# New announced durations for the list scheduler of the attention stage

## The chip, the cores and the metric

The kernel runs on one core of a Trainium2 chip, in one launch. The metric is the time on the device in microseconds (us). Lower is better. A core has a matrix engine (TensorE, PE in the profile), three engines for elementwise work (VectorE or DVE, ScalarE or ACT, GpSimd or POOL) and SyncE (SP), whose queue issues most of the transfers. Each engine works through its own queue of instructions in order, and they wait for each other by semaphores.

## The reference, cut to what matters

The input is x (16 batches of 1024 nodes with 128 features) and a 0/1 adjacency per batch. Four layers follow each other, each with a layer norm and a ReLU before it and a sum with x after it. Layer 0 thins out the adjacency row by row and applies three graph convolutions with batch norms. The other three are what the stage of this change computes:

```python
# layer 1: attention, 4 heads of 32; edges enter as log(adjacency)
scores = einsum('chqd,chkd->chqk', q, k) * SCALE + log(max(adj, EPS))
x = x + softmax(scores) @ v, projected by Wo
# layer 2: graph attention (GAT)
e = leaky_relu(s_i[i] + s_j[j]); e = where(adj > 1e-8, e, -1e9)
x = x + einsum('bijh,bihd->bjhd', softmax(e, axis=i), Wh)
# layer 3: graph convolution (GCN)
x = d^-1/2 (adj + I) d^-1/2 @ h @ W.T + b + x
```

## The kernel before, in words

A first stage thins out the adjacency, a second computes the convolutions of layer 0, and the last, `attentions_plain`, does layers 1 to 3. A slow path behind a test at the end is built into the program as well, and the test decides at run time that it is not entered.

`attentions_plain` is written as seven Python generators, each of which goes through the 16 batches:

- `matrices` loads the adjacency (tile a, from HBM by SP), turns it into fp8 (tile A, L1318 on ACT), checks on DVE that it holds 0 and 1 only (L1322) and on PE and ACT that it is symmetric (L1329 to L1335).
- `before` adds up the end of layer 0 from spilled rows (tiles h_a and hT_a, L1365 on PE, L1369 on DVE), normalizes (`normal`), transposes (`transposed`, L1291 on PE), and makes q, k (L1383) and v (`natural_times`, L1303).
- `attend` copies 16 times the adjacency into the score banks (tile t, four PSUM banks, one buffer; L1416 on ACT), multiplies the heads' keys and queries onto it (L1421 on PE) and takes the exponential in two halves (L1429 on ACT). This is done 16 times a batch.
- `values` multiplies the exponentials by v and by ones (L1452 on PE), 16 steps a batch; after each 8 it takes the reciprocal (L1458) and scales (oT, L1460, DVE). Then comes the output projection (L1303) and the sum with x (L1462).
- `positive` makes for each of the four heads a mask of the pairs with a positive score: the destination scores go out to HBM and come back spread over all partitions (tile dst), and DVE compares, 8 instructions a head (tile pm, L1503).
- `gat` normalizes, transposes, multiplies by W2 (L1523), makes the exponentials of the scores, splits the values into three bf16 parts (tiles vals and parts; POOL L1543, ACT L1549 and L1553, DVE L1551 and L1555), sums over A (L1563, 8 steps) and over the masks (L1578, 16 steps), with a DVE reduction after each (L1566, L1581), and combines the two (L1589 to L1598).
- `gcn` normalizes, splits into parts (L1615 to L1621), multiplies by A (L1632) and the identity (L1636), copies (aggT, L1639), projects (L1303) and stores the result.

Nobody writes the order of this work by hand. Before a step, a generator yields the engine, an announced duration, the planned time from which the step may start, and a change in the number of held PSUM banks of the pool "sum" (two banks). `in_order` keeps a planned free time for each engine and always takes the step with the smallest planned start, then those not on PE, then the generator with the least planned PE work done in relation to its share. The chosen generator is resumed and emits the instructions of its step. So the instructions of each queue, transfers included, stand in the order in which the planner took the steps. The core of it:

```python
engine, took, needs, _ = j["next"]
start = max([free[engine], needs] + [min(pools[pool]) for pool, change in tiles(j) if change > 0])
key = (start, engine == "PE", j["did"] / j["per"] + j["lag"])
...
end = free[engine] = start + took
...
j["next"] = j["job"].send(end + HOP)
```

HOP is 0.25. Nothing of the planned times is left in the program: no instruction waits for a clock. Two more things bind the order: `before` and `matrices` begin a batch only when `gcn` has finished the batch four earlier and `values` the one two earlier, and most tiles of `gat`, `gcn` and `before` have one buffer.

Of the kernel before, what the change touches and what calls it, by code (L numbers as in the profile page):

```python
# [1213 lines left out]
def attentions_plain(tc, x, spill, final, ready_weights, adj, deg, trouble, eye, out, scores, bound, reach):  # L1214
    nc = tc.nc
    with ExitStack() as ctx:
# [68 lines left out]
        def transposed(src, t, out):  # L1285

            for hf in range(2):
                e = yield "PE", 0.7, t, 1
                ps = bank()
                for c in range(4):  # L1290
                    nc.tensor.transpose(ps[:, c * P:(c + 1) * P], src[:, 4 * hf + c, :], ident)  # L1291
                e = yield "ACT", 0.6, e, -1
                nc.scalar.copy(out[:, hf * HN:(hf + 1) * HN], ps)
            return e

        def natural_times(xT, t, w, eng, finish):

            for hf in range(2):
                e = yield "PE", 1.05, t, 1
                ps = bank()  # L1300
                for c in range(4):
                    k = 4 * hf + c
                    nc.tensor.matmul(ps[:, c * P:(c + 1) * P], xT[:, k * P:(k + 1) * P], w, start=True, stop=True)  # L1303
                e = yield eng, 0.7, e, -1
                finish(slice(4 * hf, 4 * hf + 4), blocked(ps))
            return e

        def matrices():

            for b in range(B):  # L1310
                while done["gcn"] < b - 3 or done["attend"] < b - 1:
                    yield
                m = adp.tile([P, NB, N], F8, name="A")
                for i in range(NB):
                    t = yield "ACT", 1.3, 0.0, 0
                    a = lp.tile([P, N], F32, name="a")
                    nc.sync.dma_start(a, adj[b, i * P:(i + 1) * P, :])
                    nc.scalar.activation(m[:, i, :], a, AF.Relu, accum_out=deg[:, b, i:i + 1], saturate=False)  # L1318
                    yield "DVE", 1.4, 0.0, 0
                    junk = lp.tile([P, N], F8, name="junk", bufs=1)  # L1320

                    nc.vector.scalar_tensor_tensor(junk, a, 0.0, a, op0=ALU.is_gt, op1=ALU.not_equal,  # L1322
                                                   accum_out=trouble[:, b, i, 0:1], saturate=False)
                    for hf in range(2):
                        w = min(HN, (i - 4 * hf) * P)
                        if w > 0:
                            e = yield "PE", 0.1 + w / 1024, t, 1
                            ps = bank()
                            nc.tensor.matmul(ps[:, :w], ident16, m[:, i, hf * HN:hf * HN + w], start=True, stop=False)  # L1329
                            for j in range(w // P):  # L1330
                                nc.tensor.matmul(ps[:, j * P:(j + 1) * P], m[:, 4 * hf + j, i * P:(i + 1) * P], minus16,
                                                 start=False, stop=j == w // P - 1)
                            yield "ACT", 0.8, e, -1
                            junk = lp.tile([P, HN], BF16, name="junk2", bufs=1)
                            nc.scalar.activation(junk[:, :w], ps[:, :w], AF.Abs, accum_out=trouble[:, b, i, 1 + hf:2 + hf])  # L1335

                t = yield "DVE", 0.2, 0.0, 0
                nc.vector.tensor_scalar(dinv[:, b], deg[:, b], 1.0, None, op0=ALU.add)
                yield "POOL", 1.7, t, 0
                nc.gpsimd.tensor_tensor(dinv[:, b], dinv[:, b], minus_half, op=ALU.pow)  # L1340
                A[b] = m

        def before():

            for b in range(B):
# [6 lines left out]
                for hf in range(2):  # L1352
                    cols = slice(hf * HN, (hf + 1) * HN)
                    two = w1.tile([P, 2, HN], F32, name="h_a")
                    for l in range(2):
                        nc.sync.dma_start(two[:, l], spill[l, b][:, cols])
                    rows = [two[:, 0], two[:, 1], last[:, cols]]
                    for half in range(2):
                        e = yield "PE", 2.2, 0.0, 1 - half
                        if half == 0:  # L1360
                            ps = bank()
                            nc.tensor.matmul(ps, ones16, final[3][:, None, :].to_broadcast([3, 4, D]), start=True, stop=False)
                        for c in range(2 * half, 2 * half + 2):
                            for l in range(3):
                                nc.tensor.matmul(ps[:, c * P:(c + 1) * P], rows[l][:, c * P:(c + 1) * P], final[l],  # L1365
                                                 start=False, stop=c == 3 and l == 2)
                    t = yield "DVE", 0.7, e, -1
                    part = xt[:, 4 * hf:4 * hf + 4, :]
                    nc.vector.tensor_tensor(part, part, blocked(ps), op=ALU.add)  # L1369
                h = w1.tile([P, NB, D], F32, name="h_a")  # L1370
                t = yield from normal(xt, t, h)
                hT = w1.tile([P, N], F32, name="hT_a")
                t = yield from transposed(h, t, hT)
# [4 lines left out]
                for out_, w, bias, scale in ((qT, wq, bqc, qscale), (kT, wk_, bkc, 1.0)):  # L1378
                    for hf in range(2):
                        cols = slice(hf * HN, (hf + 1) * HN)  # L1380
                        e = yield "PE", 0.95, t, 1
                        ps = bank()
                        nc.tensor.matmul(ps, w, hT[:, cols], start=True, stop=True)  # L1383
                        e = yield "ACT", 0.7, e, -1
# [12 lines left out]
        def attend():  # L1397

            last = 0.0


            s = pss.tile([P, H, HN], F32, name="t")
            for hd in range(H):
                for c in range(4):
                    nc.tensor.matmul(s[:, hd, c * P:(c + 1) * P], ident16, ident16, start=c == 0, stop=c == 3)
            n = 0
            for b in range(B):
                while b not in ready or b not in A:
                    yield
                t, xt, qT, kT, va = ready[b]  # L1410
                for hf in range(2):
                    cols = slice(hf * HN, (hf + 1) * HN)
                    for k in range(NB):
                        e = yield "ACT", 1.9, last, 0

                        nc.scalar.activation(s, A[b][:, k, None, cols].to_broadcast([P, H, HN]), AF.Copy, scale=16.0)  # L1416
                        e = yield "PE", 1.1, max(e, t), 0

                        for hd in range(H):
                            r = slice(hd * HD, (hd + 1) * HD)  # L1420
                            nc.tensor.matmul(s[:, hd], kT[r, k * P:(k + 1) * P], qT[r, cols], start=False, stop=True,  # L1421
                                             skip_group_check=True)
                        while n > 1 and n - 2 not in taken:
                            yield
                        es = ep.tile([P, H, HN], F32, name="e")
                        e = max(e, taken.get(n - 2, 0.0))
                        for hd in range(0, H, 2):
                            e = yield "ACT", 1.07, e, 0
                            nc.scalar.activation(es[:, hd:hd + 2], s[:, hd:hd + 2], AF.Exp, scale=SIGMA)  # L1429
                        exps[n] = es, e  # L1430
                        last = e
                        n += 1

        def values():

            free, n = 0.0, 0
            for b in range(B):
                oT = w1.tile([P, N], F32, name="oT")
                for hf in range(2):
                    cols = slice(hf * HN, (hf + 1) * HN)  # L1440
                    for k in range(NB):
                        while n not in exps:
                            yield
                        es, e = exps[n]
                        e = yield "PE", 1.95, max(e, free), 0
                        if k == 0:
                            acc, den = [bank(psa, "acc") for _ in range(2)]
                        va = ready[b][4]
# [58 lines left out]
        def gat():  # L1507
            for b in range(B):
# [42 lines left out]
                nc.vector.tensor_tensor(v, v, parts[:, :, 0], op=ALU.subtract)  # L1551
                e = yield "ACT", 2.0, e, 0
                nc.scalar.copy(parts[:, :, 1], v)  # L1553
                t = yield "DVE", 2.4, e, 0
                nc.vector.tensor_tensor(parts[:, :, 2], v, parts[:, :, 1], op=ALU.subtract)  # L1555
                parts4 = parts.rearrange("p (c h) s w -> p c h s w", h=H)

# [11 lines left out]
                for hd in range(H):  # L1569
# [1 line left out]
                        yield  # L1571
                    pm, t = shared[b, hd]
                    for j in range(0, NB, 2):
                        e = yield "PE", 1.45, t, 1
                        ps = bank()
                        for jj in range(2):
                            for i in range(NB):
# [7 lines left out]
                shape = [P, NB, H, W]  # L1585
                t = yield "POOL", 3.1, e, 0
                nc.gpsimd.tensor_tensor(up, up, ex[:, 0, :, H:, None].to_broadcast(shape), op=ALU.mult)
                yield "DVE", 2.6, e, 0
                nc.vector.tensor_tensor(tot, tot, low, op=ALU.subtract)  # L1589
                nc.vector.tensor_tensor(tot, tot, ex[:, 1, :, H:, None].to_broadcast(shape), op=ALU.mult)  # L1590
                t = yield "DVE", 4.1, t, 0
# [10 lines left out]
        def gcn():  # L1602
            for b in range(B):
# [20 lines left out]
                for hf in range(2):  # L1624
                    cols = slice(hf * HN, (hf + 1) * HN)
                    for m in range(NB):
                        if m % 2 == 0:
                            e = yield "PE", 1.35, t, 0 if m else 1
                            if m == 0:
                                ps = bank()  # L1630
                        for k in range(3):
                            nc.tensor.matmul(ps, parts[:, k, m, :], A[b][:, m, cols], start=m == 0 and k == 0, stop=False)  # L1632
                    e = yield "PE", 0.8, t, 0
                    for m in range(4):
                        for k in range(3):
                            nc.tensor.matmul(ps[:, m * P:(m + 1) * P], parts[:, k, 4 * hf + m, :], ident16,  # L1636
# [191 lines left out]
```

## Time and profile before

| | us |
|---|---|
| median of 3 runs | 3990.11 |
| lowest, highest | 3984.71, 3998.74 |
| the profiled execution | 3983.57 |
| its span, first to last instruction | 3981.8 |

The mean granted clock of TensorE was 0.932 of full speed. On the page, PE is the matrix engine's multiplications and PEld its loads of the stationary operand, which overlap them. L with a number is a line of the kernel. In the timeline and the groups of instructions, `out<-in` gives the tiles by name, then the shapes, and x the number of instructions; brackets hold the idle time before and what ended it. In the list of waits the waiting engine, line and tile stand left of the arrow, and what it waited for stands right of it; the numbers are the total, the number of times and the longest. A table by stretches gives for each stretch the busy time of every engine, with the number of instructions in brackets, then the granted clock, the busy share of the transfer engines and GB/s.

### The profile page before, as it was taken

To read this page: it belongs to the slowest core of one execution; us is meant where nothing else is said; L and a number is where in the kernel's file an instruction comes from. 1 tells how busy PE (TensorE), PEld (TensorE's weight loads), DVE (VectorE), ACT (ScalarE), POOL (GpSimd) and SP (SyncE) were. 2 spreads that over 40 slices of the span, in tenths; PEclk is the share of its full clock that TensorE was granted. 3 is DMA by queue.
4 is the path that set the end of the run, shared out by engine and by line. 5 is a ranking of instruction groups with operands and counts; after the bars stand their busy time and mean duration, and the time that the engine had idled before them with its cause. 6 is when DMAs were issued, how large, how long until landed. Compare 5 with 4: busy or idle time off the path is not lost.

```text
span 3981.8 us, 65726 instructions
## 1 busy us (share of the span) xinstructions
PE 3429.2 (86%) x26692; PEld 1966.6 (49%) x26692; DVE 2528.4 (63%) x4782; ACT 2398.6 (60%) x3961; POOL 790.9 (20%) x680
## 2 busy tenths in 40 slices
PE   4888887899999986789899898998989899889775
PEld 2556565445555565335554544544444454454333
DVE  4988784553344444247775777677687686777656
ACT  3778764453333345776677676767757767776540
POOL 6545421210010011102121111111111101210110
PEclk9989986999999997999999998998999989999887
DMA  9632223443333314211221122122122112111000
GB/s 107 41 21 16 12 79 122 160 170 122 127 128 129 129 61 141 79 59 49 65 86 59 49 75 76 37 75 79 41 67 81 48 50 85 56 58 49 27 17 17
DMA packets 182499, 293.20 MB, mean 74 GB/s; under 512 B 77468, under 2 KB 124456, under 8 KB 173992
## 3 DMA queue, kind: packets, MB, share of 16 engines
q1 hardware_dynamic: 91944, 221.69, 17.1%
q0 software_dynamic: 79728, 24.66, 7.6%
q10 hardware_dynamic: 10512, 42.54, 2.7%
q8 instruction: 211, 3.46, 0.4%
q14 instruction: 104, 0.85, 0.1%
HBM read 287.98 MB, written 51.19 MB: 85 GB/s over the span
## 4 chain that ended last, share of the span: by engine, by line
PE 60%; DVE 20%; ACT 8%; DMA 5%; issue 3%; POOL 3%; ACTq 0%; SPq 0%; POOLq 0%; DVEq 0%
PE g L1040 12%; PE acc L1452 10%; PE sum L1578 9%; PE t L1421 5%; PE sum L1632 4%; PE sum L1563 4%; DVE pm L1503 3%; DMA rows<-in_adj_dram 2%; DVE rows L882 2%; PE sum L1365 2%; PE o L1089 2%; DVE r L835 2%; PE o L1090 2%; ACT e L1429 1%; PE sum L1383 1%
## 5 line engine op out<-in xcount | busy, mean ns | idle before, releaser
L1429 ACT ACTIVATE e<-t 128x1024 f32<-128x1024 f32 x512 | 507.9, 1022 | 485.8 <-PE t L1421 467.9
L1503 DVE SCALAR_TENSOR_TENSOR pm<-dst,minus,A 128x1024 fp8e4<-128x1024 f32 x512 | 675.5, 1348 | 8.4 <-DMA dst<-scores 8.3
L1040 PE MATMUL g<-C,parts 128*128 128x512 fp8e4 x2304 | 523.9, 382 | 15.9 <-DVE aggT L1042 10.0
L1416 ACT ACTIVATE t<-A 128x2048 f32<-128x2048 fp8e4 x256 | 482.0, 1883 | 3.9 <-ACT dst L1483 0.3
L1578 PEld LDWEIGHTS <-pm 128*128 128x128 fp8e4 x4096 | 346.6, 98 | 187.0 <-issue 165.0
L1578 PE MATMUL sum<-parts,pm 128*128 128x198 bf16 x4096 | 399.7, 251 | 26.1 <-DVE pm L1503 16.4
L1452 PE MATMUL acc<-e,va 128*32 128x512 f32 x2048 | 331.6, 620 | 41.1 <-ACT e L1429 38.2
L1040 PEld LDWEIGHTS <-parts 128*128 128x128 bf16 x2304 | 224.0, 99 | 264.1 <-issue 9.6
L1421 PE MATMUL t<-qT,kT 32*128 32x512 f32 x2048 | 303.5, 663 | 30.6 <-ACT t L1416 30.3
L1452 PE MATMUL acc<-e,ones_hd 128*32 128x512 f32 x2048 | 318.4, 599 | 0.0
L1581 DVE TENSOR_REDUCE pos<-sum 128x132 f32<-128x396 f32 x256 | 144.8, 566 | 201.1 <-PE sum L1578 200.5
L1563 PE MATMUL sum<-parts,A 128*128 128x396 bf16 x1024 | 212.1, 352 | 44.9 <-DVE parts L1555 24.0
L1042 DVE TENSOR_TENSOR aggT<-g,rdb 128x512 f32<-128x512 f32 x96 | 66.1, 690 | 270.6 <-PE g L1040 270.5
L1632 PE MATMUL sum<-A,gparts 128*128 128x512 fp8e4 x768 | 176.3, 382 | 24.9 <-ACT gparts L1615 17.6
L1045 POOL TENSOR_TENSOR nrm<-nrm,minus_half 128x8 f32<-128x8 f32 x48 | 78.6, 1638 | 594.3 <-DVE nrm L1103 585.9
L835 DVE TENSOR_TENSOR r<-ya,both 128x512 bf16<-128x512 f16 x184 | 140.4, 777 | 87.9 <-ACT ya L832 87.0
L1275 POOL TENSOR_TENSOR ln_st<-ln_st,minus_half 128x8 f32<-128x8 f32 x48 | 86.1, 1794 | 510.5 <-DVE ln_st L1273 348.4
L1563 PEld LDWEIGHTS <-A 128*128 128x128 fp8e4 x1024 | 94.7, 99 | 183.7 <-issue 106.6
L882 DVE SCALAR_TENSOR_TENSOR rows<-y,thirty,rows 128x1024 fp8e4<-128x1024 f16 x128 | 168.5, 1324 | 24.0 <-ACT y L874 23.5
L1100 ACT ACTIVATE sq<-o 128x512 f32<-128x512 f32 x96 | 55.2, 596 | 204.7 <-PE o L1093 125.1
L872 PE MATMUL big<-tri,rows 128*128 128x256 fp8e4 (+3 forms) x896 | 175.6, 318 | 0.6 <-ACT y L874 0.4
L885 POOL TENSOR_TENSOR own<-rows,lower 128x256 bf16<-128x256 fp8e4 x128 | 109.1, 862 | 334.2 <-DVE rows L882 201.2
(291 smaller groups left out, 6779.7 us busy)
## 6 DMA issues: line engine op xcount, KB each, us to landing
a<-in_adj_dram SPq DMA_DIRECT2D x128, 512.0 KB
C<-kept SPq DMA_DIRECT2D x48, 1024.0 KB
dst<-scores SPq DMA_DIRECT2D x64, 512.0 KB
rdb<-rdeg SPq DMA_DIRECT2D x48, 512.0 KB
spill<-hT ACTq DMA_DIRECT2D x48, 512.0 KB
kept<-rows ACTq DMA_DIRECT2D x16, 1024.0 KB
h_a<-spill SPq DMA_DIRECT2D x64, 256.0 KB
hT_a<-spill SPq DMA_DIRECT2D x16, 512.0 KB
```

The costliest lines, as they stand in the source:

```text
L835: nc.vector.tensor_tensor(r, ya, both[:, 1, :, None].to_broadcast([P, G, P]), op=ALU.is_equal)
L872: nc.tensor.matmul(ps[:, k * P:], lhs, triF[:, :HN - k * P], start=k == 0, stop=k == 3)
L882: nc.vector.scalar_tensor_tensor(row, y16, hh[:, g:g + 1], row, op0=ALU.not_equal, op1=ALU.mult, saturate=False)
L1040: nc.tensor.matmul(ps, parts[:, k, j, :], C[:, j, cols], start=j == 0 and k == 0, stop=j == NB - 1 and k == 2)
L1416: nc.scalar.activation(s, A[b][:, k, None, cols].to_broadcast([P, H, HN]), AF.Copy, scale=16.0)
L1421: nc.tensor.matmul(s[:, hd], kT[r, k * P:(k + 1) * P], qT[r, cols], start=False, stop=True, skip_group_check=True)
L1429: nc.scalar.activation(es[:, hd:hd + 2], s[:, hd:hd + 2], AF.Exp, scale=SIGMA)
L1452: nc.tensor.matmul(ps[r], ones if one else va[:, k, r], es[:, hd], start=k == 0, stop=k == NB - 1)
L1503: nc.vector.scalar_tensor_tensor(pm[:, i, :], dst[hd], minus[:, i, hd:hd + 1], A[b][:, i, :], op0=ALU.is_ge, op1=ALU.mult, saturate=False)
L1563: nc.tensor.matmul(ps[:, :3 * H * W], A[b][:, i, j * P:(j + 1) * P], parts4[:, i, :, :, W:], start=i == 0, stop=i == NB - 1)
L1578: nc.tensor.matmul(ps[:, jj * 6 * W:(jj + 1) * 6 * W], pm[:, i, (j + jj) * P:(j + jj + 1) * P], flat(parts4[:, i, hd]), start=i == 0, stop ...
L1632: nc.tensor.matmul(ps, parts[:, k, m, :], A[b][:, m, cols], start=m == 0 and k == 0, stop=False)
```

## The change

Twelve announced durations in the generators are given other values, in us. No instruction is written, removed or altered; the planner `in_order`, its shares and its start values stay.

```diff
 transposed:      - "PE", 0.7    + "PE", 0.6
 natural_times:   - "PE", 1.05   + "PE", 0.8
 matrices L1319:  - "DVE", 1.4   + "DVE", 1.32
 before L1359:    - "PE", 2.2    + "PE", 1.95
 attend L1417:    - "PE", 1.1    + "PE", 1.0
 attend L1428:    - "ACT", 1.07  + "ACT", 1.03
 values L1445:    - "PE", 1.95   + "PE", 1.85
 gat L1554:       - "DVE", 2.4   + "DVE", 2.95
 gat L1574:       - "PE", 1.45   + "PE", 1.3
 gat L1588:       - "DVE", 2.6   + "DVE", 4.1
 gcn L1628:       - "PE", 1.35   + "PE", 1.3
 gcn L1633:       - "PE", 0.8    + "PE", 0.7
```

The line in front is that of the yield; the instructions of the step follow it in the code. In `gat` the two changed DVE steps are the third part of the split (L1555) and the first two steps of the combination (L1589 and L1590).

More of the change, by code (lines that the diff above doesn't have):

```diff
@@ L1287, in transposed @@
             for hf in range(2):
-                e = yield "PE", 0.7, t, 1
+                e = yield "PE", 0.6, t, 1
                 ps = bank()
@@ L1298, in natural_times @@
             for hf in range(2):
-                e = yield "PE", 1.05, t, 1
+                e = yield "PE", 0.8, t, 1
                 ps = bank()
@@ L1318, in matrices @@
                     nc.scalar.activation(m[:, i, :], a, AF.Relu, accum_out=deg[:, b, i:i + 1], saturate=False)
-                    yield "DVE", 1.4, 0.0, 0
+                    yield "DVE", 1.32, 0.0, 0
                     junk = lp.tile([P, N], F8, name="junk", bufs=1)
@@ L1358, in before @@
                     for half in range(2):
-                        e = yield "PE", 2.2, 0.0, 1 - half
+                        e = yield "PE", 1.95, 0.0, 1 - half
                         if half == 0:
@@ L1416, in attend @@
                         nc.scalar.activation(s, A[b][:, k, None, cols].to_broadcast([P, H, HN]), AF.Copy, scale=16.0)
-                        e = yield "PE", 1.1, max(e, t), 0
+                        e = yield "PE", 1.0, max(e, t), 0
                         for hd in range(H):
@@ L1427, in attend @@
                         for hd in range(0, H, 2):
-                            e = yield "ACT", 1.07, e, 0
+                            e = yield "ACT", 1.03, e, 0
                             nc.scalar.activation(es[:, hd:hd + 2], s[:, hd:hd + 2], AF.Exp, scale=SIGMA)
@@ L1444, in values @@
                         es, e = exps[n]
-                        e = yield "PE", 1.95, max(e, free), 0
+                        e = yield "PE", 1.85, max(e, free), 0
                         if k == 0:
@@ L1553, in gat @@
                 nc.scalar.copy(parts[:, :, 1], v)
-                t = yield "DVE", 2.4, e, 0
+                t = yield "DVE", 2.95, e, 0
                 nc.vector.tensor_tensor(parts[:, :, 2], v, parts[:, :, 1], op=ALU.subtract)
@@ L1573, in gat @@
                     for j in range(0, NB, 2):
-                        e = yield "PE", 1.45, t, 1
+                        e = yield "PE", 1.3, t, 1
                         ps = bank()
@@ L1587, in gat @@
                 nc.gpsimd.tensor_tensor(up, up, ex[:, 0, :, H:, None].to_broadcast(shape), op=ALU.mult)
-                yield "DVE", 2.6, e, 0
+                yield "DVE", 4.1, e, 0
                 nc.vector.tensor_tensor(tot, tot, low, op=ALU.subtract)
@@ L1627, in gcn @@
                         if m % 2 == 0:
-                            e = yield "PE", 1.35, t, 0 if m else 1
+                            e = yield "PE", 1.3, t, 0 if m else 1
                             if m == 0:
@@ L1632, in gcn @@
                             nc.tensor.matmul(ps, parts[:, k, m, :], A[b][:, m, cols], start=m == 0 and k == 0, stop=False)
-                    e = yield "PE", 0.8, t, 0
+                    e = yield "PE", 0.7, t, 0
                     for m in range(4):
```

## The prediction

> **What bounds the kernel now.** I read the page first, then the stretches of one batch, then TensorE's waits, then the timeline at its longest waits.
>
> ```profile
> PE 3429.2 (86%) x26692; PEld 1966.6 (49%) x26692; DVE 2528.4 (63%) x4782; ACT 2398.6 (60%) x3961; POOL 790.9 (20%) x680
> ```
>
> TensorE (PE) is the busiest engine. The edits lie in the attention stage alone, from about 1545 us to the end. Cut into stretches of one batch each (the table by stretches; columns: length, then busy time of PE, PEld, DVE, ACT, POOL, the clock, DMA), it reads:
>
> ```profile
> 2560.00:2703.00 143.00, 127.59 (x968) 66.80 (x960) 100.41 (x139) 97.99 (x130) 20.75 (x11) 0.95 0.20 64
> 2847.00:2990.00 143.00, 116.07 (x869) 63.11 (x868) 105.70 (x158) 88.87 (x135) 26.19 (x13) 0.92 0.22 69
> 3850.00:3982.00 132.00, 69.84 (x438) 47.04 (x438) 76.48 (x98) 17.55 (x33) 17.44 (x10) 0.72 0.08 25
> sum 2422.00, PE 2078.11 PEld 1098.48 DVE 1635.45 ACT 1564.19 POOL 365.77; mean PE 122.24 PEld 64.62 DVE 96.20 ACT 92.01 POOL 21.52
> ```
>
> A batch takes 143 to 144 us, of which PE works 112 to 135; DVE and ACT have a quarter to spare. So over 2422 us PE is idle for 344. What it waits for, TensorE's own waits in the stage (us in total, times, longest):
>
> ```profile
> PE acc L1452 <- ACT e L1429: 38.2, 36, 4.4
> PE sum L1365 <- DMA h_a<-spill: 32.1, 17, 5.6
> PE sum L1303 <- DVE oT L1460: 31.5, 8, 9.1
> PE t L1421 <- ACT t L1416: 30.3, 20, 4.0
> PE sum L1291 <- ACT h L1282: 24.0, 2, 17.2
> PE sum L1563 <- DVE parts L1555: 24.0, 5, 12.2
> PE sum L1329 <- ACT A L1318: 21.9, 10, 6.2
> PE sum L1563 <- DVE tot L1566: 20.8, 17, 3.0
> PE sum L1632 <- ACT gparts L1615: 17.6, 1, 17.6
> PE sum L1578 <- DVE pm L1503: 16.4, 16, 2.7
> ```
>
> No row dominates: each is a place where the PE queue holds too little other work between a step and the step that needs its result through another engine. The last batch is the plainest case (PE timeline; the wait stands in brackets):
>
> ```profile
> 3854.66 3.17 PE L1291 MATMUL sum<-ident,h 128*128 128x128 f32 x8 [6.80 <-ACT h L1282]
> ...
> 3875.46 14.04 PE L1563 MATMUL sum<-parts,A 128*128 128x396 bf16 x64 [12.16 <-DVE parts L1555]
> ...
> 3951.90 0.61 PE L1632 MATMUL sum<-A,gparts 128*128 128x512 fp8e4 x1 [17.61 <-ACT gparts L1615]
> ```
>
> **What the Trainium skill says.** PSUM — Partial Sum Buffer, "Engine vs sequencer instructions": the other engines' queues are strict FIFO and matmuls start in program order. The trace agrees: at 3703 PE sat 17.19 us before gat's transposes of batch 14 (L1291), and the products of gcn behind them ran only after. Hence an announced duration acts through the order alone. TensorE: Matmul & The Clock Gate, "What's actually happening": after an idle window of about 3.4 us the array runs at half clock. The trace agrees: the output projection (L1303 from oT) takes 2.0 us a step where it follows a wait, 1.0 in steady work, so an idle us costs more than one. Perfetto Trace Analysis, "Identifying the Most-Contended Engine": matmul busy time does not measure the distance to the limit. I therefore count PE work by pitch, start to next start without idle.
>
> **The change part by part.** No instruction is added, removed or resized: both kernels have 4736 steps in the stage (PE 1584, DVE 1504, ACT 1488, POOL 160). The twelve numbers only feed the planner's greedy choice, so each edit by itself costs nothing; the order that they give together is what is priced.
>
> *Are they the trace's?* Pitches: L1421 1.07 us, L1452 1.85, L1578 1.45, L1563 1.45, L1303 1.0, L1291 0.55, L1365 about 1.65 a half step, L1383 0.96, L1632 1.3 for six, L1636 0.73, L1481 0.95, L1523 0.75, the checks at L1329 and L1331 0.42 on average. Announced 1.85, 1.3 (gcn), 0.7 agree; 1.3 for L1578, 0.8 for L1303 and 1.0 for L1421 fall below. On DVE 2.95 (row: 2.84) and 4.1 (rows: 1.73 + 2.37) come right from 0.5 and 1.5 too short. Per batch the PE announcements fall from 126.4 to 117.3; the pitches give 120.4. The old plan had PE 5% slower than its full-clock pace, the new one 3% faster. With PE fast in the plan, other chains look longer, and the planner puts more PE work ahead of the steps that end them.
>
> *What the order shows.* The steps listed with their pitches, I added the PE work between the step that starts a chain and the step that ends it ("cover"), for all 16 batches, and summed what each lacks against its need.
> - Output projection after the last value step: rden 3.36 and oT 0.69, with hops 4.3. Mean cover 2.6 before, 6.1 after (batches 2 to 13). Lacking 28 in sum before (recorded 31.5), 10.5 after: **-21**.
> - First sums of gat after w2x (L1523 to L1563). A need of 16.3 reproduces the recorded 24.0. Mean cover 17.5, after 20.6; batch 15 has 1.9, after 14.8. Lacking 7 at most after, part of it in slow clock anyway; I take 3: **-21**.
> - gat's transposes after its normalization: before, batch 14 lacks 17.2 and batch 15 6.8. After, the sums of gat 13 end earlier: batch 14 has 8.8 of cover (about 1.5 lacking), batch 15 none behind gat's last sum (17.2): **-5**.
> - Second half of `before` (L1365 behind the h_a load, 4 us): lacking 33 (recorded 32.1), after 27.5: **-5**. On SP's queue the same loads stand in nearly the same turn; the h_a load stays behind one to four loads of a.
> - Attention's turn copy, product, exp needs 5.2 us (two steps in a row at 2686.87 and 2692.04). Product to next product lacks 90 before, 82 after: **-3**.
> - Value step after its exps (2.3 needed): lacking 73 before (recorded 38.2), after 95: 22 more, of which 0.55 shows: **+12**.
> - gcn's first product after gat's last sum: cover 23.2, then 20.8, need about 20.5; the last batch has none in both: 0. POOL's few steps feed these chains and keep their waits inside the needs above.
>
> Sum: -43. The ends agree: from the same amount of remaining PE work (67.8 us) the old kernel needed about 148 us; the new needs 17.2 to gat's transposes and then the 127 us that the old took from there, about 145.
>
> *What isn't seen.* Two margins shrink. The masks (L1503) are announced 10.4 and 7.3 us of PE work ahead for heads 0 and 1, then 7.4 and 4.3; heads 2 and 3 stay at 1.6 to 1.4 and cost nothing now outside the last batch. And attention's product comes within 0.5 us of PE work behind its copy 33 times, before 15. The first I price between 0 and 1.5 us a head in 13 batches (78), the second between 0 and 18 x 1.9 = 34. I take 0 and half, 17. Below nothing the second can go by 3, as counted. -43 + 17 = -26; what half clock adds to idle time is left out, since it follows the sign.
>
> The profiled execution (3983.57) lies 6.5 us below the median of 3990.11. Against the median: 3990 - 26 = 3964; I put **3966**.
>
> **The rivals.**
> - *Covers hold* (forecast, 0.48): 3940 to 3978.
> - *ACT becomes the pace* (slower, 0.35). The new plan takes PE 3% too fast, so PE reaches attention's products and value steps just when ACT's copy or exp does, and ACT's FIFO, filled with gat's casts, is late. Price: 34 for copies + 22 for exps at full length, with 44% for half clock (a stage loss of 496 beyond 1926 of pitches against 344 recorded) 81; against gains of 52: +29, or 4019; with the masks 0.4 us late per head another 20, 4039. It decides when the added close pairs stall two thirds of their length, with that surcharge. For it: ACT's waits already lead the list. Against: ACT is 70% busy and the distance of products hardly moves.
> - *Stalls only move* (same, 0.17): what PE gains at the output projection it loses at the next wait, since DVE's masks and PSUM's two sum banks pace the batch: 3980 to 4000. Against: PE is idle 344 us for many small causes.
> - That the change does nothing is excluded: attention of batch 10 on starts while gat is half a batch further behind than before.
>
> **How the numbers follow.** About 0.3%, 12 us, is what a measurement of this kernel can tell from no change. The range runs from -43 with the half clock's 44% and a little more (3918) to the slower rival with late masks (4040). The likeliest case alone is 3940 to 3978.
>
> **What would show it.** Right: the oT and parts waits of PE fall to about 10 and 5 us each; the wait before L1291 of batch 14 goes, and one of about 17 us stands before that of batch 15; the 12.16 before L1563 there goes; batches of 141 to 142 us. Wrong: L1421 behind ACT t or L1452 behind ACT e rising together by over 40 us, or L1578 behind pm above 40, or a batch at 145.

## The result, and the profile after

| | before | after |
|---|---|---|
| median, us | 3988.45 (4 runs) | 3953.6 (4 runs, 3947.89 to 3959.44) |
| profiled execution, us | 3983.57 | 3959.44 |
| its span, us | 3981.8 | 3957.5 |

The ratio is 0.9917, 95% interval 0.9900 to 0.9934: 33 us faster, where 24 had been forecast. The page's first part of the kernel after:

```profile
PE 3428.3 (87%) x26692; PEld 1955.4 (49%) x26692; DVE 2524.1 (64%) x4782; ACT 2391.7 (60%) x3961; POOL 804.0 (20%) x680
```

The instruction counts are those of before and the busy times nearly so. The work is the same; less time lies between it. The attention stage, from 1560 us to the end, in one stretch (before: 2422 us, PE busy 2078):

```profile
sum 2398.00, PE 2084.12 PEld 1091.49 DVE 1633.87 ACT 1559.05 POOL 377.72; mean PE 2084.12 PEld 1091.49 DVE 1633.87 ACT 1559.05 POOL 377.72
```

PE is idle for 2398 - 2084 = 314 us in the stage, before 344. What it waits for now (total, times, longest):

```profile
PE acc L1452 <- ACT e L1429: 61.5, 44, 7.6
PE sum L1578 <- DVE pm L1503: 29.3, 22, 4.0
PE sum L1365 <- DMA h_a<-spill: 21.5, 15, 2.8
PE t L1421 <- ACT t L1416: 20.8, 17, 2.9
...
PE sum L1291 <- ACT h L1282: 16.4, 3, 14.7
PE sum L1291 <- ACT hT L1293: 14.5, 5, 4.6
PE sum L1523 <- ACT hT L1293: 12.5, 8, 3.2
PE sum L1329 <- ACT A L1318: 11.4, 9, 3.6
PE sum L1303 <- DVE oT L1460: 9.4, 6, 2.2
...
PE sum L1291 <- ACT junk L1335: 7.5, 3, 3.3
PE sum L1523 <- ACT h L1529: 5.1, 7, 1.4
PE sum L1291 <- ACT va L1387: 5.0, 1, 5.0
...
PE sum L1563 <- DVE parts L1555: 0.4, 1, 0.4
```

Read row by row against before: oT 31.5 to 9.4, parts 24.0 to 0.4, the h_a load 32.1 to 21.5; the exponentials 38.2 to 61.5 and the masks 16.4 to 29.3. The last two batches in the PE timeline:

```profile
3709.24 3.02 PE L1291 MATMUL sum<-ident,h 128*128 128x128 f32 x8 [0.62 <-ACT h L1282]
...
3826.51 3.17 PE L1291 MATMUL sum<-ident,h 128*128 128x128 f32 x8 [14.68 <-ACT h L1282]
...
3839.03 5.34 PE L1632 MATMUL sum<-A,gparts 128*128 128x512 fp8e4 x24
...
3851.68 3.29 PE L1563 MATMUL sum<-parts,A 128*128 128x396 bf16 x16
...
3928.53 0.61 PE L1632 MATMUL sum<-A,gparts 128*128 128x512 fp8e4 x1 [17.66 <-ACT gparts L1615]
```

In batch 14 the wait of 17.19 us before gat's transposes fell to 0.62. In batch 15 the 12.16 us before gat's first sums are gone, since gcn's products of batch 14 now stand there; the wait before gat's transposes grew from 6.80 to 14.68; the 17.6 before gcn's last products stays.

The PE timeline also shows where the gain came in. Attention's last output projection starts at 3797 us, before at 3846, so 49 us earlier. What follows it to the end takes 159 us, before 135, so 24 longer, with gat further behind attention (the distances stand under e5): half of what attention gains is lost in the tail.

### The profile page after: what moved, and what is told of

It is laid out like the page before. It is cut to its first block, busy times and chain, and to the rows that moved or that the text cites. A ratio compares the mean times of both kernels' runs of the same rounds, so it can differ in the third digit from the quotient of the medians.

```text
span 3957.5 us, 65696 instructions
## 1 busy us (share of the span) xinstructions
PE 3428.3 (87%) x26692; PEld 1955.4 (49%) x26692; DVE 2524.1 (64%) x4782; ACT 2391.7 (60%) x3961; POOL 804.0 (20%) x680
## 4 chain that ended last, share of the span: by engine, by line
PE 60%; DVE 18%; ACT 11%; DMA 5%; POOL 4%; issue 3%; SPq 0%; ACTq 0%; POOLq 0%; DVEq 0%
PE g L1040 12%; PE acc L1452 11%; PE sum L1578 8%; PE t L1421 5%; PE sum L1632 4%; PE sum L1563 4%; DVE pm L1503 3%; DMA rows<-in_adj_dram 3%; ACT e L1429 2%; PE sum L1365 2%; DVE rows L882 2%; DVE r L835 2%; PE o L1089 2%; PE o L1090 2%; DVE rden L1458 1%
## 5 line engine op out<-in xcount | busy, mean ns | idle before, releaser
L1578 PE MATMUL sum<-parts,pm 128*128 128x198 bf16 x4096 | 399.5, 252 | 42.1 <-DVE pm L1503 29.3
L1452 PE MATMUL acc<-e,va 128*32 128x512 f32 x2048 | 356.7, 633 | 64.2 <-ACT e L1429 61.5
L1452 PE MATMUL acc<-e,ones_hd 128*32 128x512 f32 x2048 | 343.5, 615 | 0.7 <-DVE oT L1460 0.7
L1421 PE MATMUL t<-qT,kT 32*128 32x512 f32 x2048 | 299.0, 654 | 21.2 <-ACT t L1416 20.8
L1563 PE MATMUL sum<-parts,A 128*128 128x396 bf16 x1024 | 203.4, 342 | 19.7 <-DVE tot L1566 17.6
L1275 POOL TENSOR_TENSOR ln_st<-ln_st,minus_half 128x8 f32<-128x8 f32 x48 | 94.6, 1970 | 446.4 <-DVE ln_st L1273 406.2
L1322 DVE SCALAR_TENSOR_TENSOR junk<-a 128x1024 fp8e4<-128x1024 f32 x128 | 159.3, 1244 | 20.5 <-DMA a<-in_adj_dram 20.2
```

Of the source, the lines that this page charges most:

```text
L1452: nc.tensor.matmul(ps[r], ones if one else va[:, k, r], es[:, hd], start=k == 0, stop=k == NB - 1)
L1563: nc.tensor.matmul(ps[:, :3 * H * W], A[b][:, i, j * P:(j + 1) * P], parts4[:, i, :, :, W:], start=i == 0, stop=i == NB - 1)
L1578: nc.tensor.matmul(ps[:, jj * 6 * W:(jj + 1) * 6 * W], pm[:, i, (j + jj) * P:(j + jj + 1) * P], flat(parts4[:, i, hd]), start=i == 0, stop ...
```

## The experiments

Three readings are tested. **Covers**: the time follows from how little PE work the order puts into the gaps that the chains leave; "lacking" is the prediction's count, summed over the six kinds of place, in us. **True numbers**: a plan on true durations is a better plan. **Luck**: any new order draws from a spread, without relation to the count. The count of each kernel e1 to e12 was made from its order before it ran; that of the kernel after was first summed when its time was known. "Measured" is the ratio of the kernel's time to that of the kernel before, with its 95% interval.

**e1, the PE edits alone.** The edits of L1288, L1299, L1359, L1417, L1445, L1574, L1628 and L1633.

> The eight edits of PE durations alone (L1288, L1299, L1359, L1417, L1445, L1574, L1628, L1633); DVE and ACT keep the old numbers. Theory of the covers: what the chains lack of PE work, counted from the order as in the prediction, is 126 us in sum here, against 175 before and 145 with all twelve; so about 49 us faster than before (3935 to 3950), a little faster than all twelve. Rival, true numbers: the DVE edits are the ones that correct real errors (0.5 and 1.5 us), so this keeps less than half of the gain (3970 to 3985). Rival, luck of the draw: any value from 3940 to 4000.

Measured: 0.9917 (0.9895 to 0.9939), 33 us faster, the same as with all twelve. The count's 49 was too much, the rival's half of the gain too little.

**e2, the other four alone.** The edits of L1319, L1428, L1554 and L1588.

> The four edits of DVE and ACT durations alone (L1319, L1428, L1554, L1588). Theory of the covers: lacking 158 us against 175, so 10 to 20 us faster than before (3965 to 3980). Rival, true numbers: these are the corrections that count, 20 to 30 us faster. Rival, luck: no relation to the count.

Measured: 0.9940 (0.9917 to 0.9964), 24 us faster. The two halves give 33 and 24, together 33: they do not add up, so no edit owns a part of the gain. The 24 us lie in the range of "true numbers" (20 to 30) and a little beyond the count's 10 to 20, whose range of times holds the measured median of 3968: this run does not tell the two apart.

**e3, the three PE numbers that had fallen below the trace.**

```diff
-  e = yield "PE", 1.3, t, 1          # L1574
+  e = yield "PE", 1.45, t, 1
-  e = yield "PE", 0.8, t, 1          # L1299
+  e = yield "PE", 1.0, t, 1
-  e = yield "PE", 1.0, max(e, t), 0  # L1417
+  e = yield "PE", 1.07, max(e, t), 0
```

> All twelve edits, but the three PE durations that fell below the trace set to the measured pitches: L1574 1.45 (not 1.3), L1299 1.0 (not 0.8), L1417 1.07 (not 1.0). Theory of the covers: lacking 169 us against 175 before, so nearly all of the gain is lost: 0 to 12 us faster than before (3973 to 3990). Rival, true numbers: a plan on true numbers is the best, so at least as fast as all twelve (3940 to 3955). Rival, luck: no relation.

Measured: 1.0011 (0.9998 to 1.0023). With numbers closer to the trace than either kernel's, the gain is gone. This is against "true numbers". PE's waits in the stage:

```profile
PE sum L1303 <- DVE dinv L1338: 29.1, 3, 9.9
PE sum L1365 <- DMA h_a<-spill: 28.0, 22, 2.8
...
PE sum L1563 <- DVE parts L1555: 17.6, 3, 12.4
PE sum L1303 <- DVE oT L1460: 14.4, 5, 5.2
```

The 12.4 before gat's first sums of the last batch is back. The first row is the output projection's as well, as DVE and PE show at one of the three places:

```profile
3430.47 0.68 DVE L1460 TENSOR_TENSOR oT<-acc,rden 128x512 f32<-128x512 f32 x1
3431.07 0.16 DVE L1338 TENSOR_SCALAR dinv<-degree 128x8 f32<-128x8 f32 x1
...
3431.30 2.05 PE L1303 MATMUL sum<-weights,oT 128*128 128x128 f32 x8 [9.61 <-DVE dinv L1338]
```

oT ends at 3431.15 and the projection starts 0.15 us later; dinv, which the list names, merely stands next to oT. So the projection waits 14.4 + 29.1 = 43.5 us here, more than the 31.5 of before.

**e4, old numbers, PE booked 7.2% shorter.** In `in_order`: `end = free[engine] = start + took * (scale if engine == "PE" else 1.0)`, scale 0.928 in this stage.

> The old numbers everywhere, but in this stage the planner counts 0.928 of each PE duration when it books the engine (126.4 us a batch become 117.3, as with the twelve edits); the PE work done that sets priorities is not scaled. Theory of the covers, in the form that a PE announced too fast makes the planner put more work ahead of chains: lacking 130 us, so about 45 us faster than before (3938 to 3955). Rival, true numbers: nothing is made truer, so no gain or a loss (3985 to 4000). Rival, luck: no relation.

Measured: 0.9936 (0.9913 to 0.9960), 25 us faster. Nothing was made truer, and most of the gain came; the size was forecast at 45.

**e5, one edit.** L1359 from 2.2 to 1.95, all else old.

> One edit of the twelve alone: L1359 from 2.2 to 1.95 on top of the old numbers. By the sum of what the chains lack: 119 us, far below the old order's 175, so 20 to 40 us faster than before (3950 to 3970), as much as all twelve. Rival, the share of PE that is announced: this takes 1 us of the 9.1 us a batch, so about a tenth of the gain (3983 to 3990). Rival, luck of the draw: anything from 3950 to 4000.

Measured: 0.9878 (0.9851 to 0.9905), 49 us faster, more than the count's 20 to 40, and at least as much as with all twelve (33; the intervals just overlap). An edit of 1 us a batch does no less than one of 9. Its distance from the output projection to gat's transposes is 14 us of PE work in the mean, near the old order's 11.5; with all twelve it is 33. So that attention runs ahead of gat, which the order shows from batch 10 on, is not needed for the gain.

**e6, another HOP.** The planner's HOP is 0.20 instead of 0.25 in this stage.

> The old durations; only the planner's HOP is 0.20 instead of 0.25 in this stage, a change with no meaning for the chip. Lacking: 174.5 us as in the old order, so no change: 3980 to 4000. Rival, the old order was just an unlucky one and any other is better: 3950 to 3975.

Measured: 0.9993 (0.9976 to 1.0009). Not every new order is better.

**e7, one of the three alone.** All twelve edits, but L1299 at 1.0.

> The twelve edits, but L1299 at its pitch of 1.0 (not 0.8). Lacking: 176 us against 145 with all twelve, so the gain goes: 3975 to 4000. Rival, the PE total announced (118.5 us a batch against 117.3) sets the gain: 3950 to 3962.

Measured: 1.0036 (1.0026 to 1.0045), 14 us slower than before. One number of twelve decides between a gain of 33 us and a loss; the total announced does not. The loss is not in the waits: PE's idle time in the stage is 348 us, before 344, and the rest of the 22 us by which the stage grew is busy time of PE (2096, before 2078), for which the count has no term.

**e8, the planner is told of two waits.** The edits of e1, and

```diff
-  e = yield "PE", 1.95, 0.0, 1 - half
+  e = yield "PE", 1.95, e + 4.0 if hf and not half else 0.0, 1 - half   # L1359
-  t = yield from natural_times(oT, free, wo, ...
+  t = yield from natural_times(oT, free + 3.0, wo, ...                  # L1462
```

> The PE edits of e1_pe_only, and two waits told to the planner that it did not know: the output projection may be planned only 3.0 us after oT's planned end (L1462), and the second half of before only 4.0 us after its first half's end, for the h_a load (L1359). Lacking: 104 us, the least of all orders counted, so 5 to 25 us faster than e1_pe_only (3935 to 3955); PE's waits for oT and for h_a near 5 us each. Rival, the gain is used up, since the clock and other waits take it back: 3955 to 3965.

Measured: 0.9867 (0.9844 to 0.9891), 53 us faster. The two rows nearly go:

```profile
PE sum L1365 <- DMA h_a<-spill: 7.9, 4, 3.4
PE sum L1303 <- DVE oT L1460: 0.4, 1, 0.4
```

**e9, one place moved by hand.** The old order was written out as a list of turns and replayed by a loop in place of `in_order`. The output projection is held until two more PE steps of other generators have gone.

> The old order, written out step by step and replayed without the planner, with one thing moved: each of the 16 output projections (L1303 from oT, with the two sums at L1462) waits until two PE steps of other generators more have gone ahead of it; what hung on it follows as soon as it can. Cover before the projection: 4.8 us in the mean, before 2.6; lacking there 6 us in sum, before 28. Theory of the covers, counted at this place alone: PE's wait for oT falls from 31.5 to about 6, and with the slow clock after waits the time falls by 25 to 35 us (3953 to 3963). Theory of the covers, counted at all places: the steps pulled ahead are partly attention's products, whose count rises from 31 to 52 us, so that the sum only falls from 175 to 169: 0 to 10 us faster (3976 to 3988). Rival, waits for oT don't matter: no change and no wait gone.

Measured: 1.0376 (1.0362 to 1.0390), 150 us slower: all three expectations missed. PE's wait for oT is gone, and this came:

```profile
PE t L1421 <- ACT t L1416: 185.7, 35, 21.4
```

The longest ones are read in the timeline; one of them, ACT and then PE:

```profile
3069.96 3.18 ACT L1282 ACTIVATE h_g<-x,ln_st 128x128 f32<-128x128 f32 x8 [12.95 <-DVE ln_st L1279]
3073.05 0.60 ACT L1615 CAST gparts<-h_g 128x512 bf16<-128x512 f32 x1
3073.56 1.87 ACT L1416 ACTIVATE t<-A 128x2048 f32<-128x2048 fp8e4 x1
...
3075.48 2.09 PE L1421 MATMUL t<-qT,kT 32*128 32x512 f32 x8 [19.09 <-ACT t L1416]
3077.51 2.74 PE L1632 MATMUL sum<-A,gparts 128*128 128x512 fp8e4 x6
3080.04 1.57 PE L1303 MATMUL sum<-weights,oT 128*128 128x128 f32 x8
```

The steps pulled ahead of the projection were the next batch's attention product and a gcn product. The attention product needs its copy, which on ACT stands behind gcn's normalization, which waits for DVE. PE sat 19.09 us with a step that was not ready, and the projection, now behind it, sat too, though its oT was done at 3065.30. Work in front of a wait covers it only if it is ready itself; the count does not see that. The traces show that the order on ACT and DVE changed as well: what hung on the projection moved with it. The old order replayed without the move was not run, so how much of the 150 us is due to the two steps alone stays open.

**e10, one wait more told to the planner.** e8, and for the third part of the split `t = 2.0 + (yield "DVE", 2.4, e, 0)` (L1554).

> e8_cover with one more wait told to the planner: the planned end of the third part of gat's split (L1555) is put 2.0 us later for what needs it, so that more PE work stands ahead of gat's first sums. Lacking 94 us, against 104 in e8_cover: 0 to 10 us faster than e8_cover, 3925 to 3938. Rival, used up: as e8_cover or slower, 3935 to 3950.

Measured: 0.9849 (0.9834 to 0.9865), a median of 3925.8, about 60 us faster than before; against e8 the intervals overlap. Its median is the lowest here. Its stage has 2362 us with PE busy 2072.08, so 290 idle:

```profile
PE t L1421 <- ACT t L1416: 40.6, 28, 4.0
PE acc L1452 <- ACT e L1429: 39.1, 42, 2.6
PE sum L1563 <- DVE tot L1566: 27.8, 25, 3.5
PE sum L1578 <- DVE pm L1503: 26.6, 24, 4.1
...
PE sum L1365 <- DMA h_a<-spill: 4.1, 4, 2.6
```

What is left leads with the attention chain and DVE. The forecast of 0 to 10 us came true, but not for its reason: e8's list has no wait of gat's first sums for the parts any more, so there was nothing to win at that place. The row that fell most is another, that of PE's transposes (L1291) behind ACT's hT (L1293), from 26.9 to 12.4.

**e11, the projection told, old numbers.** The second edit of e8 alone.

> What e9_projection_later did by hand, told to the planner instead: old numbers, but the output projection may be planned only 3.0 us after oT's planned end (L1462), and the whole stage is planned anew. Lacking: 145 us against 175, of it 16 before the projection (28). Theory of the covers: 20 to 35 us faster than before, PE's wait for oT 10 to 18 us. Rival, after e9_projection_later: any later projection makes PE wait for attention's copies, L1421 above 60 us and slower than before.

Measured: 0.9974 (0.9964 to 0.9984), 10 us faster. The wait for oT fell as counted, the time by less than the 20 to 35 counted, and a fifth of e9's trouble came with it:

```profile
PE t L1421 <- ACT t L1416: 62.9, 36, 4.0
...
PE sum L1303 <- DVE oT L1460: 9.5, 2, 9.1
```

22 us were won at the projection and 33 lost on the copies. PE's idle time still fell by 18, since the exponentials (38.2 to 25.8), the parts (24.0 to 13.3) and the h_a load (32.1 to 24.3) waited less in the new order. The rival had L1421 right and the sign wrong.

**e12, the load told, old numbers.** The first edit of e8 alone, with 2.2.

> Old numbers, but the planner knows of the h_a load: the second half of before may be planned only 4.0 us after the first half's end (L1359). Lacking: 143 us against 175, of it 14 for the load (33). Theory of the covers: 20 to 35 us faster than before, PE's wait for h_a about 10 to 15 us instead of 32.1. Rival, a load's wait only moves to another row: the wait goes, the time stays within 10 us.

Measured: 0.9898 (0.9877 to 0.9918), 41 us faster, more than the count's 20 to 35:

```profile
PE sum L1365 <- DMA h_a<-spill: 4.8, 4, 2.3
```

The row lost 27 us, and the stage's PE idle time fell from 344 to 2381 - 2069.06 = 312. The row is not the whole of it: the whole stage was planned anew, the waits for oT and the parts fell by 17 and 18 as well, and others rose. The stage fell by 41 us, more than its idle time.

All together, from the largest count to the smallest. The last two columns are of the one profiled execution of each kernel; that of e6 lies 16 us above its median:

| kernel | lacking, us | ratio to before | PE idle in the stage, us | stage, us |
|---|---|---|---|---|
| e7 | 176 | 1.0036 | 348 | 2444 |
| before | 175 | 1 | 344 | 2422 |
| e6 | 175 | 0.9993 | 338 | 2437 |
| e3 | 169 | 1.0011 | 343 | 2437 |
| e9 (by hand) | 169 | 1.0376 | 473 | 2578 |
| e2 | 158 | 0.9940 | 333 | 2407 |
| after | 145 | 0.9917 | 314 | 2398 |
| e11 | 145 | 0.9974 | 326 | 2408 |
| e12 | 143 | 0.9898 | 312 | 2381 |
| e4 | 130 | 0.9936 | 323 | 2401 |
| e1 | 126 | 0.9917 | 310 | 2398 |
| e5 | 119 | 0.9878 | 304 | 2382 |
| e8 | 104 | 0.9867 | 308 | 2372 |
| e10 | 94 | 0.9849 | 290 | 2362 |

Luck would leave no relation. The three new orders of the planner with 169 or more lie within 0.4% of before, all below 160 are faster, and the two lowest are the fastest. In between the count is rough: e4 and e11 gained less than their neighbours. It ranks the planner's orders better than it tells their size: of the twelve forecasts of time made with it, those of e1, e3, e4, e5, e9, e11 and e12 missed, and e7's came at the edge of its range.

## Why the prediction was right, point by point

**The place was right.** The change acts through the order alone, and what PE lacked in front of a chain's end is what moved. Output projection: -21 forecast, 31.5 to 9.4 is -22. gat's first sums: -21, 24.0 to 0.4 is -24. The h_a load: -5, measured -11. gat's transposes: -5, measured -8, and in the last batch the new wait of 17.2 was measured at 14.68. Of the signs that were named, those of the waits came, with the parts at 0.4 even below the 5 forecast. Of the signs of being wrong, those of the waits did not: the rows of attention's products (L1421) and value steps (L1452) together rose by 14 us and not by 40, and pm stands at 29.3. Batch lengths were not compared.

**At the projection the sum agreed better than its parts.** With a need of 4.3 us no place can lack more, but the list of before has a wait of 9.1. One of 8.12 shows what is missing:

```profile
2971.00 3.35 DVE L1458 RECIPROCAL rden<-acc 128x512 f32<-128x512 f32 x1
...
2977.14 1.22 DVE L1598 TENSOR_TENSOR x<-x,h 128x1024 f32<-128x1024 f32 x1
2978.28 0.68 DVE L1460 TENSOR_TENSOR oT<-acc,rden 128x512 f32<-128x512 f32 x1
...
2979.11 2.05 PE L1303 MATMUL sum<-weights,oT 128*128 128x128 f32 x8 [8.12 <-DVE oT L1460]
```

Between rden and oT, DVE works off the end of gat's combination. The count takes a chain at its bare length and leaves out what stands before its steps in the other engine's queue. That 28 counted came near 31.5 recorded is in part luck, and with it that the -21 came true.

**Three terms were mis-sized.** The value steps behind the exponentials cost 23 more, not 12: the factor 0.55, which the old order's record gave, did not hold for the new pairs. Attention's products behind their copies were put at -3 and then, as half of an unseen cost, at +17; they fell by 9.5. The masks, put at nothing between 0 and 78, cost 13.

**One cost was not in the sum.** The transposes of gat and of `before` and the W2 products now wait for ACT's copies and checks (hT, va, junk, h; rows L1291 and L1523): 14.5 + 12.5 + 7.5 + 5.1 + 5.0 = 45 us, before about 6. That they come close behind each other in the new order could be read from the list: the mean PE work between the transposes and the W2 products falls from 1.7 to 0.8 us. Many small rows, the checks at L1329 among them (21.9 to 11.4), gave 32 back. Recorded idle time fell by 30 in all, the profiled execution by 24 and the medians by 35. The forecast of -26 came out close partly by luck, because these errors cancel.

**The reason given was half right.** That a PE announced too fast makes the planner put more work ahead of chains is supported once, by e4. But e5 gains at least as much as all twelve with nearly the old total, and e7 loses it all with nearly the new one. The announced total is no lever: each number reshuffles 4736 steps, and the sign is known only once the order is counted. Why the planner lands on these orders stays open.

**One reading was off.** A batch's stretch has PE at work for 112 to 136 us (136.38 is the highest), and for 103 in the first stretch; the forecast does not rest on it.

**The rivals.** The slower rival's mechanism, PE held by ACT, was at work: the row of the exponentials and those of ACT's copies and checks (the 45 us above) together rose by 62, but by short waits and not at attention's copies, and the covers outweighed it. e9 shows what it costs where it does decide. That stalls only move was true in part of e11, and not of the change.

## What to carry to other kernels

A list scheduler's numbers should be judged by the order that they give: list the steps, put measured pitches on them, and count the work between each step and the one that ends its chain. The count ranks orders; it does not tell their time. Truer durations are not by themselves a better order. Telling the planner of the waits that it does not know (a load of 4 us, a chain's end) gained 41 us (e12) and 10 us (e11) on the old numbers, and took the 33 us of e1 to 53 (e8). But one duration changed by 0.25 gained 49 (e5), so that telling beats any other reshuffling that lowers the count is not shown. And don't move a step by hand in one queue: what is pulled in front of it has to be ready on the other engines too.

## What the runs showed of the hardware

On TensorE a wait can cost more than its length. The stage of before and of e8, in one stretch each:

```profile
1560.00:3982.00 2422.00, 2078.11 (x15316) 1098.48 (x15316) 1635.45 (x2416) 1564.19 (x2128) 365.77 (x192) 0.93 0.19 60
1560.00:3932.00 2372.00, 2063.50 (x15297) 1084.93 (x15297) 1626.97 (x2406) 1561.51 (x2128) 370.47 (x192) 0.95 0.20 61
```

In e8 PE's idle time fell by 36 us and the stage by 50, in e12 by 32 and 41. The granted clock rose from 0.93 to 0.95 in e8 and to 0.94 in e12, and PE's busy time fell (2078 us, then 2064 and 2069) although the matmuls are the same. e9's timeline shows one such step: the attention product behind the wait of 19.09 us takes 2.09 us, in steady work 1.14, and the clock granted there is 0.50:

```profile
3075.00:3079.00 4.00, 3.52 (x12) 1.09 (x13) 2.41 (x3) 2.87 (x5) 0.56 (x1) 0.50 0.00 0
```

This is no fixed rate. In the kernel after, idle time fell by 30 us and the stage by 24 only, since PE's busy time rose by 6 at a clock of 0.94; why it rose is open. A straight line through the thirteen orders of the planner in the table gives, as an estimate, 1.36 us of stage for 1 us of idle time.
